# Lending idle streams' PSUM banks in a four-layer graph attention kernel, with a shorter subtraction and transposes tile by tile

## The chip, the cores and the metric

The kernel runs on one core of a Trainium2 chip. The metric is the device time of one execution in microseconds (us), from the start of the program to its end. Times of one kernel are given as the median of several executions.

## The reference

The input is `x`, 32 graphs of 512 nodes with 256 features, and one adjacency matrix of 512 x 512 for all of them. Four layers follow each other; all arithmetic is in 32-bit floats. In every layer the nodes are normalised, clipped at zero, sent through an attention over the graph, and added back:

```python
h = jnp.maximum(_layernorm(x, axis=-1), 0.0)
x = x + _L0_gnn_ref(h, adj, L0_gnn_W, L0_gnn_a)
# layers 1, 2, 3 in the same way

def _layernorm(x, axis=-1, eps=1e-5):
    m = jnp.mean(x, axis=axis, keepdims=True)
    v = jnp.var(x, axis=axis, keepdims=True)
    return (x - m) / jnp.sqrt(v + eps)

def _L0_gnn_ref(h, adj, W, a):          # layers 1 and 2 differ in slope, heads and output function
    Wh = jnp.einsum('bnf,fo->bno', h, W)
    s_i = Wh @ a1
    s_j = Wh @ a2
    e = jax.nn.leaky_relu(s_i[:, :, None] + s_j[:, None, :], negative_slope=LEAKY_ALPHA)
    e = jnp.where(mask[None, :, :], e, -jnp.inf)
    attention = jax.nn.softmax(e, axis=-1)
    h_prime = jnp.einsum('bij,bjo->bio', attention, Wh)
    return jax.nn.elu(h_prime)
```

Layer 2 has four heads of 64 features. Layer 3 is a chain: a dense layer to 512 features, an attention over all nodes without a mask, a dense layer back to 256 features, and an attention with the mask.

## The kernel before

**Tiles and stages.** One graph is a batch `b`. Its nodes lie on the 128 partitions, in four tiles of 128 nodes (`NT = 4`); its 256 features make two blocks of 128 (`KF = 2`). Per layer the stages are:

- `norm` (L255 to L277), for two node tiles at a time: mean and variance on DVE (L262, L263), the inverse deviation `rs` on ACT (L265, L266), and then `xn` on DVE. With `late` set, which is so after layers 0 and 1, `xn` is max(x - mean, 0) in one instruction with two operations (L269), and the factor `rs` is applied later, in `values`. Without it, `xn` is (x - mean) * rs (L273).
- `turn_pair` (L277 to L283): four transposes on TensorE (L70) bring two node tiles of `xn` into one PSUM tile `b`, and one ACT instruction evicts them with relu into `hT` (L283). The two loops run over feature blocks outside and over the two node tiles inside.
- `values` (L301 to L318): per node tile two matmuls (L66) into a PSUM tile, evicted by ACT with the exponential of the scores (L312, L315) and a scaled copy (L313, L318) into `v`.
- `weights`: four transposes spread a column of `v` over the partitions, and DVE makes the four tiles of attention weights `w` (L346).
- `averages` and `aggregate`: matmuls of `w` and `v` into a PSUM tile, which ACT evicts after a reciprocal on DVE (L380): L414, L415 and L433 in layers 0 and 1, L692 and L693 at the end of layer 3.

In layer 3 the attention without a mask is done by sorting (`sort_attend`), with indirect DMAs issued by POOL (L600, L648) and prefix sums on DVE (L618 to L639) and TensorE (`tot`, `before`). Only the last batch does it by plain matmuls (`attend`).

**Streams.** Four streams (`NS = 4`) work on different batches at the same time: stream i takes the batches i, i + 4, i + 8 and so on. A stream is a Python generator that stops at points where its next work would have to wait, and yields an estimated due time. At build time a loop takes the stream with the smallest due time, and so writes down the program order. Stream i begins at `i * LEAD`, with `LEAD = 75`. A fifth generator, `setup`, is woven into the start: it transposes the adjacency mask (`own` to `maskT`) and prepares the weights of the later layers (`finish_w` and `project`: transposes of a weight, a copy `wT` on ACT at L114, two to four matmuls, a copy on DVE at L120). From the program order the language's scheduler makes a fixed order for each engine, in which an instruction can be put ahead of one whose inputs or whose buffer it expects later. [...]

**PSUM.** All PSUM tiles come from one helper. There are eight tiles, and each stream has two of its own, under a tag that only this stream uses:

```python
def bank():
    return psum.tile([P, N], FP, tag=f"b{turn[0]}", name="b", bufs=8 // NS)
```

`turn[0]` is the number of the stream whose code is being written down; while `setup` runs it is 3, and in the loop over `own` it goes 3, 2, 1, 3. A stream that has not begun, or that has ended, leaves its two tiles unused.

Of the kernel before, what the change touches and what calls it, by code (L numbers as in the profile page):

```python
# [19 lines left out]
FP = mybir.dt.float32  # L20
# [4 lines left out]
OP = mybir.AluOpType  # L25
# [3 lines left out]
P = 128  # L29
# [6 lines left out]
def fast(ctx, tc, flag, x, adj, w0, a0, w1, a1, w2, a2, mlp1_w, mlp1_b, mlp2_w, mlp2_b,  # L36
         w_fc, a_fc, w_hand, a_hand, out):
    nc = tc.nc
    B, N, F = x.shape
    NT = N // P  # L40
    KF = F // P
# [4 lines left out]
    NS = 4  # L46
# [6 lines left out]
    psum = ctx.enter_context(tc.tile_pool(name="psum", bufs=1, space=bass.MemoryType.PSUM))  # L53
    dram = ctx.enter_context(tc.tile_pool(name="dram", bufs=1, space=bass.MemoryType.DRAM))

    turn = [0]
# [11 lines left out]
    def transpose(p, x, i, tied=False):  # L68
        spent[0] += 2 * P
        instruction = nc.tensor.transpose(p, x, i)  # L70
        if tied:
            tc.keep_in_program_order(instruction)

    def bank():
        return psum.tile([P, N], FP, tag=f"b{turn[0]}", name="b", bufs=8 // NS)


    nc.scalar.preload_act_table_set("natural_log_exp_and_others")
# [28 lines left out]
    def project(dst, block, k, a_cols):  # L107

        ft, n = a_cols.shape[1], a_cols.shape[2]
        p = bank()  # L110
        for f in range(ft):
            transpose(p[:, f * P:(f + 1) * P], block(k, f), ident)
        wT = work.tile([P, N], FP, tag="y", name="wT", bufs=3)
        nc.scalar.copy(wT[:, :ft * P], p[:, :ft * P])  # L114
        q = bank()
        for f in range(ft):
            matmul(
                q[:, :n], wT[:, f * P:(f + 1) * P], a_cols[:, f, :], start=(f == 0), stop=(f == ft - 1)
            )
        nc.vector.tensor_copy(dst, q[:, :n] if len(dst.shape) == 2 else q[:, :n].rearrange("p (h c) -> p h c", c=3))  # L120
# [79 lines left out]
    def setup():  # L200
# [7 lines left out]
        for j in range(NT):  # L208
            turn[0] = NS - 1 - j % (NS - 1)
            p = bank()  # L210
            for t in range(NT):
                transpose(p[:, t * P:(t + 1) * P], own[:, t, j * P:(j + 1) * P], ident, j + t == 0)
            nc.scalar.copy(maskT[:, j, :], p)
# [36 lines left out]
    def small(shape, name):  # L250
        return work.tile([P] + shape, FP, tag=name, name=name, bufs=2 * NS)
# [4 lines left out]
    def norm(xt, xn, rs, t0, late):  # L256


        st = small([2, 6], "st")
        mv = small([2, 2], "mv")  # L260
        for i in range(2):
            nc.vector.bn_stats(st[:, i, :], xt[:, t0 + i, :])  # L262
            nc.vector.bn_aggr(mv[:, i, :], st[:, i, :])  # L263
        rp = rs[:, t0:t0 + 2]
        nc.scalar.activation(rp, mv[:, :, 1], AF.Ln, bias=eps)  # L265
        nc.scalar.activation(rp, rp, AF.Exp, scale=-0.5)  # L266
        for i in range(2):
            if late:
                nc.vector.tensor_scalar(  # L269
                    xn[:, t0 + i, :], xt[:, t0 + i, :], mv[:, i, 0:1], 0.0, op0=OP.subtract, op1=OP.max  # L270
                )
            else:
                nc.vector.tensor_scalar(  # L273
                    xn[:, t0 + i, :], xt[:, t0 + i, :], mv[:, i, 0:1], rp[:, i:i + 1], op0=OP.subtract, op1=OP.mult
                )

    def turn_pair(xn, hT, t0):  # L277
        p = bank()
        for k in range(KF):
            for i in range(2):  # L280
                c = (k * 2 + i) * P
                transpose(p[:, c:c + P], xn[:, t0 + i, k * P:(k + 1) * P], ident)
        nc.scalar.activation(hT[:, :, t0 * P:(t0 + 2) * P], p.rearrange("p (k n) -> p k n", k=KF), AF.Relu)  # L283

    def turned(xn, when):

        hT = work.tile([P, KF, N], FP, tag="hT", name="hT", bufs=3)
        turn_pair(xn, hT, 0)
        yield when
        turn_pair(xn, hT, 2)  # L290
        yield after_us(0.6)
        return hT
# [114 lines left out]
    def layer0(xt, xn, rs, when):  # L407
        v, wt = yield from plain((yield from turned(xn, when)), W0)
        xn, rs = new_xn(), small([NT], "rs")
        for t0 in range(0, NT, 2):  # L410
            r, q = pair(), pair("q")
            for i in range(2):
                p, rd = averages(v, wt, t0 + i)
                nc.scalar.activation(q[:, i, :], p, AF.Exp, scale=rd)  # L414
                nc.scalar.activation(r[:, i, :], p, AF.Relu, scale=rd)  # L415
                if i == 0:
                    yield after_us(0)
            add_elu(xt[:, t0:t0 + 2, :], r, q)
            norm(xt, xn, rs, t0, True)
            last, when = when, after_us(6)  # L420
            if t0 == 0:
                yield after_us(0)
        yield last
        return xn, rs, when

    def layer1(xt, xn, rs, when):
        v, wt = yield from plain((yield from turned(xn, when)), W1, rs)
        xn, rs = new_xn(), small([NT], "rs")
        for t0 in range(0, NT, 2):
            r = pair()  # L430
            for i in range(2):
                p, rd = averages(v, wt, t0 + i)
                nc.scalar.activation(r[:, i, :], p, AF.Relu, scale=rd)  # L433
                if i == 0:
                    yield after_us(0)
            xr = xt[:, t0:t0 + 2, :]
            nc.vector.tensor_tensor(xr, xr, r, op=OP.add)
            norm(xt, xn, rs, t0, True)
            last, when = when, after_us(5)
            if t0 == 0:  # L440
                yield after_us(0)
        yield last
        return xn, rs, when

    def layer2(xt, xn, rs, when):
# [56 lines left out]
        for t0 in range(0, NT, 2):  # L502
            norm(xt, xn, rs, t0, False)
# [244 lines left out]
    while ready:  # L748
        i = min(ready, key=ready.get)
        if i == NS:  # L750
            turn[0] = NS - 1
            ready[i] += 4.0
            if next(early, early) is early:
                del ready[i]
            continue
        turn[0], spent[0] = i, 0.0
        begun[0] = ready[i]
        wait = next(streams[i], None)
        if wait is None:
            del ready[i]  # L760
        else:
            ready[i] = wait

# [409 lines left out]
@with_exitstack  # L1173
def kernel(ctx: ExitStack, tc: tile.TileContext, *args):
    nc = tc.nc
    keep = ctx.enter_context(tc.tile_pool(name="keep", bufs=1))
    flag = keep.tile([1, 1], I32, name="flag")
    fast(tc, flag, *args)
    bad = nc.values_load(flag[0:1, 0:1], min_val=0, max_val=1)
    with tc.If(bad > 0):  # L1180
        general(tc, *args)
# [27 lines left out]
```

## The time and the profile before

| | |
|---|---|
| median of three executions | 2951.32 us (2948.66 to 2954.25) |
| the profiled execution | 2955.39 us |
| its span, first to last instruction | 2953.7 us |
| TensorE matmuls (PE) busy | 2870.6 us (97%) |
| DVE busy | 2224.6 us (75%) |
| ACT busy | 1538.9 us (52%) |
| POOL busy | 497.2 us (17%) |
| mean granted TensorE clock | 0.994 |

The profile shows one execution, the profiled one, which took 4.07 us more than the median. PE stands for matmuls and transposes on TensorE, PEld for the loading of their stationary operand, DVE for VectorE, ACT for ScalarE, POOL for GpSimd, SP for the engine that issues most DMAs. A line such as L66 is the line of the kernel: L66 is the helper that issues all matmuls, L70 the one that issues all transposes. "Idle before" is the time in which an engine did nothing ahead of an instruction, put down to what released it. PEclk is the clock granted to TensorE, as a share of its full speed.

### The profile page before, as it was taken

What the parts mean: (1) busy time and instruction counts of PE and PEld (TensorE: products, weight loads), DVE (VectorE), ACT (ScalarE), POOL (GpSimd) and SP (SyncE); (2) the same over time, 40 slices, a digit from 0 to 9 for tenths busy, and PEclk for the clock granted to TensorE, in tenths of its full rate; (3) what the DMA queues carried; (4) which work ended last, traced back from release to release, by engine and by line L of the source; (5) the groups of instructions that cost most, each with busy time, mean ns of one, the idle gap of its engine ahead of it and who ended that gap; (6) DMA issues with size and microseconds to landing.
All of it is one profiled execution on the core that took longest, in us unless ns stands there. A gap on an engine that the chain in (4) does not pass through costs nothing.

```text
span 2953.7 us, 43083 instructions
## 1 busy us (share of the span) xinstructions
PE 2870.6 (97%) x15177; PEld 2329.4 (79%) x15177; DVE 2224.6 (75%) x5674; ACT 1538.9 (52%) x3918; POOL 497.2 (17%) x509
## 2 busy tenths in 40 slices
PE   7999999999999999999999999999999999999998
PEld 5778888778887877888778888778878778887765
DVE  4578878778878777878778777787777788777763
ACT  3445555554555555555545555545555555555544
POOL 0011122111122121121111121111121111221120
PEclk9999999999999999999999999999999999999999
DMA  3033233233232332233332232222232322332330
GB/s 93 12 100 95 83 98 115 82 99 98 83 101 96 99 101 91 85 106 94 101 94 87 87 115 92 96 97 91 87 116 90 98 94 86 94 115 76 98 108 16
DMA packets 193150, 270.89 MB, mean 92 GB/s; under 512 B 16992, under 2 KB 156062, under 8 KB 192928
## 3 DMA queue, kind: packets, MB, share of 16 engines
q1 hardware_dynamic: 163168, 169.76, 18.4%
q0 software_dynamic: 29760, 98.30, 10.2%
q8 instruction: 123, 2.02, 0.3%
q14 instruction: 99, 0.81, 0.1%
HBM read 152.62 MB, written 115.39 MB: 91 GB/s over the span
## 4 chain that ended last, share of the span: by engine, by line
PE 80%; DVE 12%; ACT 5%; issue 1%; DMA 1%; POOL 0%; SPq 0%; POOLq 0%; ACTq 0%; DVEq 0%
PE b L66 72%; PE b L70 7%; DVE st L262 3%; DVE xn L273 1%; DVE xn L269 1%; DVE sums L634 1%; ACT v L318 1%; DVE sums L625 1%; DVE x L399 1%; ACT rs L265 1%; DVE y L398 1%; DVE mv L263 1%; DVE y L703 1%; ACT y L498 1%; ACT q L497 0%
## 5 line engine op out<-in xcount | busy, mean ns | idle before, releaser
L66 PE MATMUL b<-v,w 128*128 128x65 f32 (+1 forms) x7232 | 1221.6, 321 | 11.0 <-DVE w L346 8.5
L66 PEld LDWEIGHTS b<-v,w 128*128 128x128 f32 x7232 | 1050.1, 191 | 175.1 <-issue 66.0
L66 PE MATMUL b<-WFC,oT 128*128 128x256 f32 (+1 forms) x2048 | 499.6, 381 | 3.0 <-ACT ends L521 3.0
L66 PEld LDWEIGHTS b<-WFC,oT 128*128 128x128 f32 x2048 | 375.0, 190 | 52.0 <-ACT v L522 3.4
L66 PE MATMUL b<-W,hT 128*128 128x259 f32 (+1 forms) x1536 | 384.6, 389 | 5.0 <-ACT v L318 4.4
L346 DVE SCALAR_TENSOR_TENSOR w<-b,v,maskT 128x512 f32<-128x512 f32 x512 | 370.2, 747 | 4.6 <-PE b L70 3.4
L600 POOL DMA_INDIRECT order<-v,at x248 | 280.3, 1130 | 490.2 <-DVE oT L719 152.4
L66 PEld LDWEIGHTS b<-W,hT 128*128 128x128 f32 x1536 | 284.8, 191 | 55.7 <-ACT v L318 10.7
L346 DVE SCALAR_TENSOR_TENSOR w<-spread,v,maskT 128x512 f32<-128x512 f32 x384 | 270.1, 746 | 0.0
L380 DVE RECIPROCAL rden<-b 128x1 f32<-128x1 f32 (+1 forms) x516 | 79.6, 166 | 252.6 <-PE b L66 250.8
L706 POOL TENSOR_TENSOR x<-x,y 128x512 f32<-128x512 f32 x64 | 81.1, 1268 | 1076.3 <-ACT y L704 962.8
L66 PE MATMUL b<-hT,WM 128*128 128x512 f32 x512 | 249.1, 597 | 0.7 <-ACT hT L283 0.7
L648 POOL DMA_INDIRECT g<-table,at x124 | 121.2, 977 | 732.5 <-ACT y L668 380.9
L66 PE MATMUL b<-oT,WM 128*128 128x512 f32 x512 | 231.4, 595 | 0.0
L522 ACT ACTIVATE v<-b,ends 128x256 f32<-128x256 f32 x256 | 119.0, 468 | 179.0 <-PE b L66 174.5
L262 DVE BATCH_NORM_STATS2 st<-x 128x6 f32<-128x256 f32 x512 | 192.9, 408 | 5.2 <-DMA x<-in_x_dram 2.6
L283 ACT ACTIVATE hT<-b 128x512 f32<-128x512 f32 x256 | 147.2, 592 | 91.3 <-PE b L70 91.2
L332 ACT ACTIVATE oT<-b,bias 128x512 f32<-128x512 f32 x128 | 87.8, 686 | 195.4 <-PE b L66 195.4
L405 DVE TENSOR_TENSOR y<-q,y 128x512 f32<-128x512 f32 x192 | 132.7, 691 | 67.4 <-ACT q L404 66.5
L70 PE MATMUL b<-ident,xn 128*128 128x128 f32 x1024 | 154.9, 279 | 23.9 <-DVE xn L273 18.0
L66 PEld LDWEIGHTS b<-oT,WM 128*128 128x128 f32 x512 | 97.6, 191 | 95.8 <-issue 92.5
L70 PEld LDWEIGHTS b<-ident,xn 128*128 128x128 f32 x1024 | 125.4, 144 | 59.8 <-DVE xn L273 33.5
(142 smaller groups left out, 3749.1 us busy)
## 6 DMA issues: line engine op xcount, KB each, us to landing
table<-sums SPq DMA_DIRECT2D x62, 1032.0 KB
sums<-order SPq DMA_DIRECT2D x62, 516.0 KB
spread<-row SPq DMA_DIRECT2D x96, 256.0 KB
x<-in_x_dram SPq DMA_DIRECT2D x32, 512.0 KB
out_dram<-x SPq DMA_DIRECT2D x64, 256.0 KB
sums<-order SPq DMA_DIRECT2D x62, 129.0 KB
order<-v,at POOLq DMA_INDIRECT x248, 2.9
g<-table,at POOLq DMA_INDIRECT x124, 4.7
```

The source lines that it names most:

```text
L66: nc.tensor.matmul(p, w, x, **flags)
L70: instruction = nc.tensor.transpose(p, x, i)
L262: nc.vector.bn_stats(st[:, i, :], xt[:, t0 + i, :])
L283: nc.scalar.activation(hT[:, :, t0 * P:(t0 + 2) * P], p.rearrange("p (k n) -> p k n", k=KF), AF.Relu)
L332: nc.scalar.activation(o[:, f, :], p, AF.Relu, bias=bias[:, f:f + 1])
L346: w = nc.vector.scalar_tensor_tensor(wt[:, j, :], r, t_col(j), maskT[:, j, :], op0=OP.max, op1=OP.mult)
L380: nc.vector.reciprocal(r, den)
L405: nc.vector.tensor_tensor(r, q, r, op=OP.add)
L522: nc.scalar.activation(halves[c][:, t, :F], ps[:, :F], AF.Copy, scale=ends[:, t, 0:1])
L600: nc.gpsimd.indirect_dma_start(out=orders[c], out_offset=bass.IndirectOffsetOnAxis(ap=at[:, 0, t:t + 1], axis=0), in_=halves[c][:, t, :], ...
L648: nc.gpsimd.indirect_dma_start(out=g, out_offset=None, in_=table, in_offset=bass.IndirectOffsetOnAxis(ap=at[:, 1, t:t + 1], axis=0),)
L706: nc.gpsimd.tensor_tensor(xr, xr, y, op=OP.add)
```

## The change

Four edits, all in `fast`:

1. `bank` hands out PSUM tiles from the stream's own tag and, in turn, from the tags of all streams that are not active. A stream counts as active from the first time that the loop takes it until its generator ends. `setup` is never counted. While all four streams are active, a stream gets its own tag only, as before.
2. With `late` set, `xn` is x - mean alone; the clip at zero that it had is left to the relu in the eviction of `turn_pair`, which was there before.
3. The loops of `turn_pair` are exchanged: both transposes of the first node tile come first, then both of the second.
4. The loop that takes the streams keeps the set `active`.

```diff
+    active = set()
+    banks = [0]
+
     def bank():
-        return psum.tile([P, N], FP, tag=f"b{turn[0]}", name="b", bufs=8 // NS)
+
+        own = [turn[0], *(i for i in range(NS) if i not in active and i != turn[0])]
+        banks[0] += 1
+        return psum.tile([P, N], FP, tag=f"b{own[banks[0] % len(own)]}", name="b", bufs=8 // NS)
...
             if late:
                 nc.vector.tensor_scalar(
-                    xn[:, t0 + i, :], xt[:, t0 + i, :], mv[:, i, 0:1], 0.0, op0=OP.subtract, op1=OP.max
+                    xn[:, t0 + i, :], xt[:, t0 + i, :], mv[:, i, 0:1], None, op0=OP.subtract
                 )
...
     def turn_pair(xn, hT, t0):
         p = bank()
-        for k in range(KF):
-            for i in range(2):
+        for i in range(2):
+            for k in range(KF):
                 c = (k * 2 + i) * P
                 transpose(p[:, c:c + P], xn[:, t0 + i, k * P:(k + 1) * P], ident)
...
         begun[0] = ready[i]
+        active.add(i)
         wait = next(streams[i], None)
         if wait is None:
             del ready[i]
+            active.remove(i)
         else:
             ready[i] = wait
```

## The prediction

> **What bounds the kernel now.** I read the busy shares first, then stretches of the span, then the waits of TensorE in each stretch, then the timeline around the longest ones. The page says that matmuls fill the span:
>
> ```profile
> PE 2870.6 (97%) x15177; PEld 2329.4 (79%) x15177; DVE 2224.6 (75%) x5674; ACT 1538.9 (52%) x3918; POOL 497.2 (17%) x509
> ```
>
> The change adds and removes no matmul, so it can only touch the 83 us in which PE is idle, and the time lost to a lower TensorE clock. Four stretches show where these lie (start : end and length, then busy us of each engine with instruction counts, then PEclk):
>
> ```profile
> 0.00:225.00 225.00, 195.58 (x1030) 160.19 (x1031) 135.65 (x388) 95.05 (x257) 17.51 (x26) 0.95 0.22 69
> 225.00:2800.00 2575.00, 2542.26 (x13539) 2070.95 (x13538) 2006.76 (x5107) 1375.29 (x3513) 457.53 (x463) 1.00 0.30 95
> 2800.00:2944.20 144.20, 132.77 (x611) 98.27 (x610) 80.34 (x178) 67.41 (x149) 20.92 (x19) 0.96 0.20 64
> 2944.20:2953.70 9.50, 0.00 (x0) 0.00 (x0) 1.80 (x4) 1.12 (x2) 1.26 (x1) 0.61 0.14 45
> ```
>
> PE idles 29.4 us while the streams start (0 to 225 us), 32.7 us in the 2575 us when all four run (1.3%), 11.4 us while they end, and 9.5 us behind the last matmul. Only the start and the end have idle streams, and only there is the clock below full. The waits of PE in the first 225 us (us in total, times, longest):
>
> ```profile
> PE b L66 <- DVE w L346: 4.4, 5, 2.6
> PE b L66 <- DVE tot L622: 3.4, 1, 3.4
> PE b L66 <- DVE W0a L104: 2.9, 1, 2.9
> PE b L70 <- ACT rs L265: 2.6, 1, 2.6
> PE b L66 <- ACT wT L114: 2.5, 5, 0.7
> PE b L70 <- DVE xn L269: 2.4, 1, 2.4
> ```
>
> Most are waits for data; `wT` L114 is ACT, through which the preparation of the weights goes, with two banks at a time. [...] Here are the stretch with the wait of 2.6 us at 65 us, and the next one:
>
> ```profile
> 64.00:68.00 4.00, 1.35 (x9) 1.03 (x8) 2.87 (x12) 1.81 (x6) 0.00 (x0) 1.00 0.00 0
> 68.00:72.00 4.00, 3.94 (x14) 2.70 (x13) 2.96 (x12) 1.58 (x7) 0.00 (x0) 0.61 0.00 0
> ```
>
> After it the clock is 0.61 for 4 us: (1 - 0.61) x 3.94 = 1.5 us more. Counted in the same way, the start loses 8.5 us of clock (at 28, 44 to 52, 68 and 176 us) and the end 4.9 us (at 2820, 2844 and 2872 us).
>
> [...]
>
> **The change part by part.**
>
> *x - mean in one operation (256 on DVE).* The price is shown by L623, which is a one-operation tensor_scalar with a column scalar, 258 elements:
>
> ```profile
> L623 DVE TENSOR_SCALAR sums<-sums,T x62: 344/350/356, 185.7 to 2847.5; 128x258 f32<-128x258 f32 x62
> L269 DVE TENSOR_SCALAR xn<-x,mv x256: 318/345/1431, 38.0 to 2791.3; 128x256 f32<-128x256 f32 x128
> ```
>
> 350 against 345 ns: no gain (ends: 0.03 us less or more each). Even 256 x 0.03 = 8 us of DVE would lie beside PE, because L269 makes PE wait only once, at 104 us. The relu costs nothing: L283 does it already. I take 0.
>
> *Transposes by tile.* With all four streams running, PE waits 16.3 us in 28 cases for `xn` L273, one per batch. The four L273 follow each other at 0.38 us; a transpose step on PE is about 0.11 us. Where four transposes stand together in the order, the second waits for the second tile today; later the first two run on tile one, which saves 0.11. The built order has this for two of four batches. In one it changes "transpose, matmul, three transposes" to "four transposes, two matmuls", which loses the filler (about 0.13); in one nothing changes. Sum 2 x 0.11 - 0.13 = 0.1 us per four batches, 0.6 us over seven rounds (-1 to +1.5).
>
> *The banks.* The built orders of the two programs agree from about 200 to 2750 us on every engine but for those transposes; SP's order is the same throughout and POOL's nearly so. What moves is the start and the end. I walk along PE's new order with the durations of the trace.
>
> - To 26 us: the weight transposes of `W0` no longer wait for two banks, so the first `values` could start 1.5 us earlier. But the mask needs `adj` (landed 11.3), L203 (1.23) and POOL (1.92), and L346 still stands behind the 2.27 us reduction L219 on DVE. I take 0.5 us of 4.2.
> - 32 to 56 us: the waits for `wT` and for L415 (0.74 + 0.51 + 0.24 + 0.73 + 0.52 = 2.7) are waits for banks, and the clock loses 3.0 there. Six lent banks remove most of it, but eight more weight transposes (0.157) and four more small matmuls (0.29) now stand ahead of stream 0's last aggregates: 2.4 us later for its chain. From +5.7 to -2.4; I take 3.0.
> - 65 us: two matmul groups of layer 2 (0.87) go into the wait of 2.65, splitting it in two short ones[...]. 0.9 to 2.4; I take 1.4.
> - 102 to 109 us: four groups of stream 1's `values` (4 x 0.43) go ahead of the transposes that wait 2.41 and 1.22. I take 1.7 (0 to 3).
> - 173 us: one `values` group goes ahead of the wait of 3.37 for `tot`, one during it (0.87), and DVE makes `tot` ahead of L399. The next transposes then wait for L269 as before. I take 1.5 (0.5 to 4, with the clock).
>
> Sum of the start 8.1. A stall that is filled can return at the next data wait, so I count 6 (0 to 13). It then carries to the end: in the middle PE is the bound, and its short waits depend on DVE and ACT work just before.
>
> - The end. At 2837 PE waits 0.66 for a bank; the order now has all eight matmuls of that stage in a row (0.4). At 2869.9 it waits 2.97 for a bank behind ACT L521; a fourth group (1.73) fits now, but the gathers (4.7 us to landing) feed the transposes of `y` behind it, so I count 1.0 (0 to 4). At 2938 and 2940.8 the last two groups wait 0.69 and 0.73 for banks, and a transpose group (0.44) stands between; now four groups follow each other. The last one ends some 2.4 us earlier and the eviction chain with it; I take 2.0.
>
> Sum of the end 3.4 (1 to 7).
>
> **Sum:** 6 + 3.4 + 0.6 + 0 = 10 us. Against the profiled execution, 2955.4 - 10 = 2945.4; that one lies 4.07 above the median, so for the median 2951.3 - 10 = **2941.3 us**.
>
> **Rivals.**
> 1. *Idle streams' banks hide little.* The start is bound by stream 0's chain through DVE and ACT: of the six waits shown, five are for DVE or for `rs`. Then only the end counts: 3.4 + 0.6 - 1 = 3 us, 2948 us. For it speaks that work put into a wait for data doesn't end that wait; against it, that the lent banks let another stream's work in, which is then gone later.
> 2. *Slower: lent work blocks PE's queue.* At 32 to 45 us the weight preparation goes ahead of stream 0's aggregates (2.4 us); two matmul groups ahead of layer 2's aggregates at 100 us and again at 173 us add 0.87 each, and a lent bank that is evicted late makes its owner wait. If this chain sets the start, it loses 4.1 us[...]: 7.3 us, with nothing won at the end, 2958 us. It decides once stream 0's delay is larger than the 2.7 us of bank waits removed.
> 3. *Clock kept.* [...]most of the 8.5 us of clock comes back too: 13 + 5 = 18 us, 2933 us.
>
> **How the numbers follow.** A difference of 0.2%, 5.9 us, is about what a measurement of this kernel can tell from no change. Chances: forecast 0.55, clock kept 0.15, little hidden 0.22, slower 0.08. Half-way between forecast and rival 1 is the bound for "faster" (2945.4), so a small part of each falls on the other's side: faster 0.70, same 0.22, slower 0.08. The range from 2932 to 2951 holds the forecast, its unknown ends, rival 1 and most of rival 3.
>
> **What would show it.** In the profile after: the middle stretch idles PE 32 us again; L269 keeps a median near 345 ns; the waits for `wT` L114 nearly vanish; those of 2.65, 2.41 and 3.37 us shrink and the clock at 44 to 52 us is near full; at the end the waits for L693, L703 and L312 are gone, that for L521 is below 1.5 us. I am wrong if the four streams' middle changes length by more than 3 us, if stream 0's second layer starts later than at 57 us, or if waits for lent banks appear.

## The result and the profile after

| | before | after |
|---|---|---|
| median, ten executions each | 2952.47 us | 2942.65 us (2940.53 to 2945.59) |
| ratio after to before | | 0.9966 [0.9959, 0.9974] |
| the profiled execution, and its span | 2955.39, 2953.7 us | 2945.59, 2943.9 us |
| mean granted TensorE clock | 0.994 | 0.995 |

In square brackets stand 95% intervals, in round ones the lowest and the highest execution. The change gains 10 us of 2952. Beside the experiments the changed kernel was run again: 0.9975 [0.9965, 0.9985], 7.4 us. The two together give about 9 us.

Code lines of the changed kernel lie 6 higher than those of before: L346 is L352, L269 is L275, L273 is L279, L312 and L318 are L318 and L324, L405 is L411. The page's line of busy times, and then the stretches of the profiled execution after (start : end, length, busy us of PE, PEld, DVE, ACT, POOL with counts, PEclk):

```profile
PE 2863.2 (97%) x15177; PEld 2326.1 (79%) x15177; DVE 2224.0 (76%) x5674; ACT 1537.4 (52%) x3918; POOL 501.3 (17%) x509
```

```profile
0.00:225.00 225.00, 200.97 (x1088) 165.72 (x1089) 143.51 (x407) 97.50 (x264) 20.28 (x28) 0.98 0.23 71
225.00:2800.00 2575.00, 2540.87 (x13527) 2069.05 (x13526) 2004.73 (x5104) 1378.82 (x3521) 459.30 (x463) 1.00 0.30 96
2800.00:2934.40 134.40, 121.36 (x566) 91.39 (x564) 74.36 (x163) 60.00 (x134) 20.47 (x18) 0.96 0.19 63
```

The same 15177 matmul records are there. In the first 225 us PE now does 1088 of them and not 1030, and idles 24.0 us in place of 29.4. In the middle it idles 34.1 us (32.7 before). The waits of PE in the first 225 us after (us in total, times, longest):

```profile
PE b L66 <- ACT hT L289: 5.3, 9, 0.9
PE b L66 <- DVE w L352: 5.2, 6, 2.7
PE b L70 <- DVE xn L279: 2.9, 4, 1.2
PE b L70 <- DVE xn L275: 2.5, 4, 1.1
PE b L66 <- ACT wT L120: 0.5, 2, 0.3
```

The single long waits for `tot` (3.4) and `rs` (2.6) are gone, and in their place stand many short ones: nine for `hT`, none above 0.9 us. The timeline of PE shows how the old waits of 2.65, 2.41 and 3.37 us look now:

```profile
61.12 1.17 PE L66 MATMUL b<-W,hT 128*128 128x268 f32 x4 [0.82 <-ACT hT L289]
62.86 0.70 PE L70 MATMUL b<-ident,xn 128*128 128x128 f32 x4 [0.57 <-DVE xn L275]
64.25 1.17 PE L66 MATMUL b<-W,hT 128*128 128x268 f32 x4 [0.69 <-ACT hT L289]
...
100.36 0.70 PE L70 MATMUL b<-ident,xn 128*128 128x128 f32 x4 [0.70 <-DVE xn L275]
101.98 2.02 PE L66 MATMUL b<-W,hT 128*128 128x259 f32 x8 [0.92 <-ACT hT L289]
...
170.60 0.44 PE L70 MATMUL b<-ident,xn 128*128 128x128 f32 x2 [1.06 <-DVE xn L275]
```

Each wait is cut into pieces with work between them. The two stretches that answer to those of 64 to 72 us before keep the full clock behind 1.83 us of idle time:

```profile
60.00:64.00 4.00, 2.17 (x11) 1.15 (x9) 3.43 (x14) 2.07 (x6) 0.00 (x0) 1.00 0.02 4
64.00:68.00 4.00, 3.75 (x20) 2.93 (x21) 3.10 (x10) 2.56 (x9) 0.00 (x0) 1.00 0.00 0
```

**One pair of profiles misleads.** Read alone, this pair puts 8.3 us ahead of batch 4 (it begins at 390.80 and not at 399.14 us) and some 2 us at the end; the expectations below, written from this pair, take 8.5 and 2.4. But the profiled execution before had a late transfer at its very beginning (PE waits 2.9 us for `W0a`), and the one after had one at its end, as shown below. The experiments gave twelve more profiles, in which most stages occur both with and without lending. I therefore cut each into four stages that begin at the same instruction in all of them, and leave out what stands ahead of the first: the first transpose of `own`, the 32 aggregates of stream 0's second layer, and SP's transfer of `row` (one for each batch) for batch 4 and for batch 31. The table has the mean, and the lowest and highest of each group in brackets, in us.

| stage | banks not lent in it | banks lent in it | difference | forecast |
|---|---|---|---|---|
| `own` to stream 0's second layer | 41.1 (5 profiles, 40.7 to 41.4) | 40.0 (6, 37.7 to 42.8) | -1.1 | -3.0 |
| second layer to batch 4 | 342.4 (6, 342.0 to 342.8) | 338.2 (8, 336.2 to 340.2) | -4.2 | -4.6 |
| batch 4 to batch 31 | 2404.0 (6, 2403.4 to 2404.4) | 2404.9 (8, 2403.5 to 2405.6) | +0.9 | -0.6 |
| batch 31 to the end | 149.7 (6, 148.5 to 151.5) | 145.1 (8, 142.3 to 148.3) | -4.6 | -3.4 |

For batch 4 to 31 a kernel counts as lent if its streams borrowed at the start. In the first row `no_setup` counts as not lent, since its preparation keeps to two banks, and the three kernels with an early reduction, below, are left out. The sum is -9.0 us, which is the time measured. The split between the first two rows is less firm than their sum: in `after_again` and `end_two` the first stage loses 6.8 us to a lower clock and the second none, in `banks_only` it is 2.6 and 3.4. (The clock's loss is half of PE's busy time while the granted clock is 0.50: in a row of matmuls of 257 columns the next one then follows after 0.428 us in the median of the first profile after, and after 0.217 at 1.00.) The forecast of the first two stages is its parts 3.0, and 1.4 + 1.7 + 1.5.

### The profile page after: what moved, and what is told of

It is laid out like the page before. It is cut to its first block, busy times and chain, and to the rows that moved or that the text cites. A ratio compares the mean times of both kernels' runs of the same rounds, so it can differ in the third digit from the quotient of the medians.

```text
span 2943.9 us, 43065 instructions
## 1 busy us (share of the span) xinstructions
PE 2863.2 (97%) x15177; PEld 2326.1 (79%) x15177; DVE 2224.0 (76%) x5674; ACT 1537.4 (52%) x3918; POOL 501.3 (17%) x509
## 3 DMA queue, kind: packets, MB, share of 16 engines
q0 software_dynamic: 29760, 98.30, 10.1%
## 4 chain that ended last, share of the span: by engine, by line
PE 77%; DVE 13%; ACT 5%; DMA 3%; issue 1%; POOL 0%; SPq 0%; POOLq 0%; ACTq 0%; DVEq 0%
PE b L66 70%; PE b L70 7%; DVE st L268 3%; DVE xn L279 1%; DMA order<-v,at 1%; DVE xn L275 1%; DVE sums L640 1%; DVE w L352 1%; ACT v L324 1%; DMA sums<-order 1%; DVE sums L631 1%; ACT y L504 1%; DVE x L405 1%; ACT q L503 1%; DVE y L404 1%
## 5 line engine op out<-in xcount | busy, mean ns | idle before, releaser
L352 DVE SCALAR_TENSOR_TENSOR w<-b,v,maskT 128x512 f32<-128x512 f32 x512 | 369.0, 743 | 4.9 <-PE b L70 3.6
L352 DVE SCALAR_TENSOR_TENSOR w<-spread,v,maskT 128x512 f32<-128x512 f32 x384 | 269.3, 741 | 0.0
L712 POOL TENSOR_TENSOR x<-x,y 128x512 f32<-128x512 f32 x64 | 81.3, 1270 | 1074.9 <-ACT y L710 963.8
L411 DVE TENSOR_TENSOR y<-q,y 128x512 f32<-128x512 f32 x192 | 132.5, 690 | 67.0 <-ACT q L410 66.5
```

Source lines behind the costliest of these rows:

```text
L352: w = nc.vector.scalar_tensor_tensor(wt[:, j, :], r, t_col(j), maskT[:, j, :], op0=OP.max, op1=OP.mult)
L411: nc.vector.tensor_tensor(r, q, r, op=OP.add)
L712: nc.gpsimd.tensor_tensor(xr, xr, y, op=OP.add)
```

## The experiments

All have the kernel before run beside them on the same chip. Theory 1 at the outset was: the gain is the lent banks', mostly at the start (8.5 us), the transposes give 0.6 us, the subtraction nothing. The rivals stand in the expectations.

**The four edits apart.** `banks_only` is the kernel before with edits 1 and 4; `sub_only` and `trans_only` are the kernel before with this alone:

```diff
# sub_only
-                    xn[:, t0 + i, :], xt[:, t0 + i, :], mv[:, i, 0:1], 0.0, op0=OP.subtract, op1=OP.max
+                    xn[:, t0 + i, :], xt[:, t0 + i, :], mv[:, i, 0:1], None, op0=OP.subtract
# trans_only
-        for k in range(KF):
-            for i in range(2):
+        for i in range(2):
+            for k in range(KF):
```

> The kernel before with edits 1 and 4 alone: idle streams' banks are lent; the subtraction keeps its two operations and the transposes their old order. Theory 1 (the lent banks bring the gain at the start and the end, the transposes about 0.6 us, the subtraction nothing): about 9 us below before, 0.5 us above the changed kernel, so 2943 us. Theory 2 (a good part comes from the shorter subtraction or from the order of the transposes): 4 us or more above the changed kernel, 2946 us or more.

> The kernel before with edit 2 alone: x - mean in one operation. Theory 1: no change, within 1.5 us of before; DVE's median of one subtraction stays at 345 ns. Theory 2: 3 us or more below before.

> The kernel before with edit 3 alone: transposes by node tile. Theory 1: 0.6 us below before (-1 to +1.5 gained), which is hardly more than the scatter; stretch 225 to 2800 us with 0.1 us less for each round of four batches. Theory 2: 3 us or more below before.

Measured: `banks_only` 0.9969 [0.9957, 0.9981], 9.2 us below before; `sub_only` 0.9994 [0.9985, 1.0002]; `trans_only` 0.9998 [0.9990, 1.0007]. The lent banks alone give the whole gain. Neither of the other edits gives a difference that the times resolve; the interval of `sub_only` still reaches to 4.4 us below before, so there the trace decides. For the transposes a stage resolves more than the whole: batch 4 to 31 takes 2403.39 us in `trans_only` against 2404.10 and 2404.07 in before and `sub_only`, 0.7 us less, as forecast. But among the other kernels whose streams don't borrow there, the two with edit 3 take 2403.4 (`setup_only`) and 2404.4 us (`end_only`), and the one without it 2404.4 (`before_early`). So 0.6 us fits, and is not shown. The subtraction's rows, of `sub_only` and then of the changed kernel (minimum, median, maximum in ns):

```profile
L269 DVE TENSOR_SCALAR xn<-x,mv x256: 318/344/1434, 35.6 to 2788.8; 128x256 f32<-128x256 f32 x128
```

```profile
L275 DVE TENSOR_SCALAR xn<-x,mv x256: 317/344/1435, 40.6 to 2783.9; 128x256 f32<-128x256 f32 x128
```

One operation less changes the median from 345 to 344 ns, that is, by nothing.

**Start and end apart.** In `start_only` an ended stream stays active; in `end_only` all streams are active from the beginning:

```diff
# start_only
-            active.remove(i)
# end_only
-    active = set()
+    active = set(range(NS))
```

> The changed kernel, but a stream that has ended stays active, so that banks are lent only before a stream begins. Theory 1: the start keeps its 8.5 us and the end loses its 2.4 us: 2945 us, 2.4 us above the changed kernel, with the waits for ACT at the two last groups of the final stage back (0.7 us each). Theory 3 (the end gains nothing on balance, because the bank wait of 2.17 us ahead of `tot` and the lower clock behind it eat it): within 1 us of the changed kernel.

> The changed kernel with all four streams counted as active from the beginning, so that banks are lent only after a stream has ended. Theory 1 (start and end add up: all of the lending gave 9.2 us, the start's share alone 4.8): 4.4 us below before. Theory 4 (they don't add up: time gained at the start is lost again at the end unless the end lends too): 2 us or less below before. The start shows the waits of before (2.6 us at 65 us, 3.4 us for `tot` at 173 us).

Measured: `start_only` 0.9984 [0.9977, 0.9991], 4.8 us below before (2949.26 against 2954.11 us); `end_only` 0.9982 [0.9975, 0.9989], 5.3 us. The first expectation missed: the end is worth as much as the start, and the split of the first pair of profiles falls. The second holds: 4.8 and 5.3 make 10.1 us, so within their intervals the two add up, and nothing gained at the start is lost again at the end.

The last stage shows best what the end gains. The four groups of eight aggregates on PE, and an instruction of the eviction chain on DVE, in the kernel before and in the changed one:

```profile
2932.57 4.32 PE L66 MATMUL b<-v,w 128*128 128x257 f32 x16 [0.98 <-DVE w L346]
2938.02 2.00 PE L66 MATMUL b<-v,w 128*128 128x257 f32 x8 [0.69 <-ACT y L693]
2940.76 2.00 PE L66 MATMUL b<-v,w 128*128 128x257 f32 x8 [0.73 <-DVE y L703]
2943.51 0.43 DVE L403 TENSOR_SCALAR q<-q 128x512 f32<-128x512 f32 x1 [0.54 <-ACT q L692]
```

```profile
2924.66 7.21 PE L66 MATMUL b<-v,w 128*128 128x257 f32 x32 [0.45 <-DVE w L352]
...
2932.58 1.26 POOL L712 TENSOR_TENSOR x<-x,y 128x512 f32<-128x512 f32 x1 [11.57 <-ACT y L710]
2932.89 1.23 DVE L409 TENSOR_SCALAR q<-q 128x512 f32<-128x512 f32 x1 [0.17 <-ACT q L698]
```

With other banks free the 32 matmuls run in one row. From the first of them to the end of the last the kernel before takes 2942.76 - 2932.57 = 10.2 us, the changed one 7.2: 3.0 us less. To the end of the span it is only 21.1 against 19.2, 1.9 us less. The evictions now come closer together, and DVE's L409 (L403 before) runs into POOL's L712: 1.23 us and not 0.43. It is 1.23 in the second profile of the changed kernel and in `banks_only` too, with L712 beginning 0.31 to 0.32 us ahead of it in all three, and 0.43 in `start_only`, whose L712 begins 2.01 us ahead and is done. This takes 0.8 of the 1.1 us that are lost again behind PE.

The other part of the end's gain lies in the 46 us ahead of this stage. From the first of the last 32 matmuls `b<-oT,WM` (2886.38 us before, 2881.13 after) to the 32 aggregates it takes 46.19 us in all six profiles without lending at the end and 43.53 to 43.55 in all eight with it: 2.65 us less for 182 matmuls in each, at full clock. Waits of PE there add up to 1.9 us before and to 0.5 after. Two of those before, which are gone:

```profile
2915.53 2.00 PE L66 MATMUL b<-v,w 128*128 128x257 f32 x8 [0.26 <-ACT y L693]
2927.51 3.50 PE L66 MATMUL b<-WHA,rT 128*128 128x259 f32 x14 [0.49 <-ACT rT L332]
```

From batch 31 to that point the two groups take 82.4 and 82.3 us on average, the second with four transposes (0.44 us) more: hardly a gain.

**A second profile of the changed kernel.**

> The changed kernel once more, for a second profile and on the chip of the next three. 9 to 10 us below before. Theory A (the bank wait of 2.17 us ahead of `tot` at 2831 us, with the lower clock behind it, comes with the built order): the wait is there again, over 1.5 us. Theory B (it comes from a gather that landed late in that one run): the wait is under 0.5 us, and batch 31 to the end takes 144 us and not 148.

Measured: 0.9975 [0.9965, 0.9985], 7.4 us; from batch 31 to the end 143.9 us, where the first profile took 148.3. The bank wait of 2.17 us ahead of `tot` is gone. Lines of PE, DVE and ACT of the first profile, in which `tot` (PE) waits for an eviction on ACT that stands behind L503, which waits for `y` of L496 on DVE, which stands behind L626, which waits for a gather:

```profile
2827.72 0.43 DVE L626 TENSOR_TENSOR sums<-sums 128x258 f32<-128x258 f32 x1 [2.34 <-DMA sums<-order]
2829.19 0.63 ACT L503 ACTIVATE q<-y 128x512 f32<-128x512 f32 x1 [6.82 <-DVE y L496]
2830.90 0.92 PE L66 MATMUL b<-tot,before 128*128 128x258 f32 x2 [2.17 <-ACT v L318]
```

And of the second, where the gather came 1.0 us earlier, although PE was 1.1 us later at the matmuls ahead of `tot`:

```profile
2826.76 0.43 DVE L626 TENSOR_TENSOR sums<-sums 128x258 f32<-128x258 f32 x1 [0.95 <-DMA sums<-order]
2828.23 0.63 ACT L503 ACTIVATE q<-y 128x512 f32<-128x512 f32 x1 [4.77 <-DVE y L496]
2829.94 0.70 PE L66 MATMUL b<-tot,before 128*128 128x258 f32 x2
```

Both signs of Theory B came true: it was one late gather. From its issue to L626 it took 5.1 us in the first profile, 3.7 in the second and 3.3 to 4.7 in the six others that lend at the end. The bank that `tot` was waiting for had been handed out, and the queues of DVE, ACT and PE carried the delay on: these instructions stand in the same order in both profiles, and L626, L503 and `tot` are each 0.96 us later in the first.

**Who borrows at the start.** In `no_setup` the preparation of mask and weights keeps to its own tag, and in `setup_only` it alone borrows:

```diff
# no_setup: preparing[0] is True only while setup is written down
+        own = own[:1] if preparing[0] else own
# setup_only
+        own = own if preparing[0] else own[:1]
```

> The changed kernel, but the preparation of mask and weights keeps to its own two banks; the streams still borrow. Theory 1 (the part of 32 to 56 us in the sum, the waits for `wT` and the clock there, is half of the start's gain): 3 us above the changed kernel, waits for `wT` of 0.5 to 0.7 us back (2.5 us in all). Theory 5 (the preparation was only ahead or behind in the same queue; the start is bound by stream 0's chain, and what helps is the streams' own borrowing at 65, 102 and 173 us): within 1 us of the changed kernel.

> The changed kernel, but only the preparation of mask and weights borrows; the streams keep to their own two banks throughout, at the end too. Theory 1 (waits for `wT` and the clock at 32 to 56 us are half of the start's gain): 3 us below before and 0.6 more from the transposes, 3.6 us. Theory 5 (only the streams' own borrowing helps at the start): 0.6 us below before, with the waits of 2.65 us for rs, 2.41 us for xn and about 3 us for tot as before.

Measured: `no_setup` 0.9969 [0.9957, 0.9981], 9.2 us below before and so equal to the changed kernel within some 4 us, which alone doesn't exclude the 3 us of Theory 1; `setup_only` 0.9998 [0.9990, 1.0006], 0.6 us below before. The forecast of 3.6 us for `setup_only` lies outside its interval (3.0 below to 1.8 above), and Theory 5 fits both kernels. Waits of PE in the first 225 us of `setup_only`:

```profile
PE b L66 <- DVE tot L630: 2.9, 1, 2.9
PE b L70 <- ACT rs L273: 2.6, 1, 2.6
PE b L70 <- DVE xn L277: 2.4, 1, 2.4
PE b L66 <- ACT wT L122: 2.3, 5, 0.5
```

The waits at 65, 102 and 173 us are all there. So are five waits for `wT`, 2.3 us in all against 2.5 before, though the preparation has six more banks; only the wait of 0.74 us for L415 is gone. Lent to the streams alone, in `no_setup`, the waits for `wT` grow to 4.9 us. Only where both borrow do they nearly go (0.5), because other work then stands between a copy and the matmul that needs it. But even that gains little: in the changed kernel waits for `hT`, `v`, `maskT` and `xn`, some 2 us in all from `own` to the second layer, stand in their place. And `no_setup`, in which PE idles 8.1 us there, more than in any other profile, loses only 1.4 us of clock, less than any other; so its waits cost no time that the runs resolve.

The second layer to batch 4 tells the same: 342.3 us in `setup_only`, 338.4 in `no_setup`. The idle time of PE in that stage is 15.0 to 15.8 us in the six profiles whose streams don't borrow, and 12.2 to 12.7 in the eight others; the clock's loss is 4.2 to 4.8 us against 0 to 3.4. The stage begins with the 32 aggregates of stream 0's second layer, which show that part of what two banks cost isn't seen as idle time. In `end_only`, whose streams keep two banks here, and in the changed kernel:

```profile
53.55 7.79 PE L66 MATMUL b<-v,w 128*128 128x257 f32 x32 [0.94 <-DVE w L352]
```

```profile
52.66 7.21 PE L66 MATMUL b<-v,w 128*128 128x257 f32 x32 [0.85 <-DVE w L352]
```

The row takes 7.79 us in `setup_only` too and 7.21 in `no_setup`, so it is the stream's own borrowing that shortens it, by 0.6 us. The trace shows where: DVE finishes the four tiles of `w` 0.66 us apart. With two banks PE does two matmuls with each tile and then waits for the next one: in the kernel before, whose row begins at 56.77 us and takes 7.79 us as well, tiles are ready at 57.29, 57.95 and 58.60 us, and every second matmul starts right behind, at 57.34, 58.00 and 58.66. With more banks it does four matmuls with each tile, which take 0.87 us, and DVE keeps ahead. The page counts these short waits as busy.

**Lending at the end only later.** In `end_two` nothing is lent while just one stream has ended:

```diff
+        own = own[:1] if len(ended) == 1 else own
```

> The changed kernel, but at the end banks are lent only once two streams have ended. Theory A: `tot` stands ahead of part of the eight matmuls of layer 3 again and waits 0.7 us or less, 1.5 to 3 us below the changed kernel. Theory B: nothing gained there, and the wait of 2.9 us for L527 is back: 1 to 2 us above the changed kernel.

Measured: 0.9971 [0.9958, 0.9983], 8.6 us below before, which is the changed kernel's own gain. From batch 31 to the end it takes 142.3 us, the lowest of the eight with lending, but `both_early`, which has the same rule, takes 146.6. Since the wait that it was to remove was one late gather's, this tells nothing more; the wait for L527 did not come back either.

**The stall that is left at the start.** Stream 0's first aggregates wait 2.73 us at 26 us, because the attention weights L352 stand on DVE behind a reduction of the whole adjacency matrix (L225, 2.28 us), which nothing needs so early. `reduce_early` moves it behind the load of the matrix:

```diff
+        tc.keep_in_program_order(nc.vector.tensor_reduce(differ[:, 0:1], adj_sb, AX.XY, OP.min))
         for j in range(NT):
             turn[0] = NS - 1 - j % (NS - 1)
...
-        tc.keep_in_program_order(nc.vector.tensor_reduce(differ[:, 0:1], adj_sb, AX.XY, OP.min))
```

`both_early` is this and `end_two` together; `before_early` is this move in the kernel before.

> The changed kernel with the reduction of the adjacency matrix on DVE (2.27 us, L225) put right behind its load, and so ahead of stream 0's first attention weights by more than the wait. If the stall of 2.73 us at 26 us and the clock of 0.69 and 0.50 behind it (2.6 us) are due to it: 2 to 5 us below the changed kernel, and the wait for w at the first aggregates below 1 us. If DVE is then late with the first normalisation instead, which stands behind the reduction: within 1 us of the changed kernel, with a wait for `xn` of about 2 us ahead of it.

> The changed kernel with both: the reduction of the adjacency matrix right behind its load, and lending at the end only once two streams have ended. If the two add up (6 us at the start, 1 to 2 us at the end): 15 to 16 us below before, 7 us below the changed kernel. If time saved at the end is only moved into the next wait for the gathers: as the kernel with the early reduction, 14 us below before. Profile: first wait for w 0.8 us, waits for `y` L411 at the end two and not four.

> The kernel before with the early reduction alone, nothing lent. Theory 1 (without lent banks PE has nothing to put into the waits at 65, 102 and 173 us, but the first stall is the same DVE reduction in both kernels): 4 to 6 us below before, so that the two changes add up. Theory 6 (what is gained ahead of 30 us is taken back by the bank waits of the preparation at 32 to 56 us): 2 us or less below before.

Measured: `reduce_early` 0.9952 [0.9938, 0.9966], 14.2 us below before; `both_early` 0.9954 [0.9941, 0.9967]; `before_early` 0.9993 [0.9985, 1.0001], 2.1 us. The lines of DVE and PE, of the changed kernel and of `reduce_early`:

```profile
23.47 2.28 DVE L225 TENSOR_REDUCE differ<-adj 128x1 f32<-128x2048 int32 x1
25.66 2.72 DVE L352 SCALAR_TENSOR_TENSOR w<-b,v,maskT 128x512 f32<-128x512 f32 x4
26.46 2.94 PE L66 MATMUL b<-v,w 128*128 128x257 f32 x6 [2.73 <-DVE w L352]
```

```profile
10.10 2.28 DVE L214 TENSOR_REDUCE differ<-adj 128x1 f32<-128x2048 int32 x1
22.05 2.73 DVE L352 SCALAR_TENSOR_TENSOR w<-b,v,maskT 128x512 f32<-128x512 f32 x4 [0.21 <-PE b L70]
22.85 2.87 PE L66 MATMUL b<-v,w 128*128 128x257 f32 x12 [0.84 <-DVE w L352]
```

The wait falls from 2.73 to 0.84, and this kernel is 5.8 us faster than the changed one run beside it (2938.42 against 2944.18 us; five and nine executions, so the size is rough). From `own` to the second layer PE idles 3.7 us, where the kernels with lending idle 5.1 to 6.3. So about 2 us of the gain are seen; the rest may be the clock or lie within the two intervals. `both_early`, 13.6 us below before, is no faster than `reduce_early`, and four waits for `y` stand at the end, not two: the later lending adds nothing. In the kernel before, Theory 6 gave the right size, but its mechanism is not seen. 1.85 us of the first wait go; from 32 to 56 us the waits for `wT` stay at 2.0 us and the one for `y` grows from 0.7 to 1.0. The one profile even keeps 3 us up to batch 4; it is of one of the fastest of 14 executions, so the interval, which reaches to 4.4 us, leaves open how much is kept.

## Why the prediction was right, and where not

The time came out as forecast (10 us; 10.0 and 7.4 measured), by the mechanism that it names: work of other streams goes into the waits of the start and the end. That the sum fits so well is partly luck, because terms that were too large and gains that it did not have make up for each other. By its steps:

- **The subtraction at nothing: right.** A row of another line with one operation was enough to price it.
- **The transposes at 0.6 us: not contradicted**, 0.7 us in `trans_only`, but the kernels that share the stage scatter by 1 us.
- **To 26 us, 0.5: not seen.** The first aggregates begin at 23.6 to 24.4 us in `sub_only`, `trans_only` and `end_only`, and at 23.6 to 26.5 in the five profiles in which streams and preparation borrow and the reduction is late; before and `sub_only`, which do not differ there, lie 2.5 us apart.
- **The preparation at 32 to 56 us, 3.0: wrong**, 1.1 us. That the waits for `wT` and L415 would go came true; that the time would go with them did not. The banks were only part of the reason for `wT`, other waits took their place, and idle time from `own` to the second layer is 6.3 to 6.4 us in before, `sub_only`, `trans_only` and `end_only`, and 5.1 to 6.3 with lending. The clock's loss, 4.5 to 4.9 us in those four, scatters from 2.6 to 8.2 with lending: it did not hang on these waits (see the last section).
- **65, 102 and 173 us, 1.4 + 1.7 + 1.5 = 4.6: right as a sum**, 4.2 us measured for the stage, 3 of them idle time. Its parts are not: cut at the transfers of `row` for batches 1 and 2, the first two waits gave 1.7 us (3.1 forecast) and the third 2.8 (1.5). Behind the wait for `tot` the clock lost 2.5 to 3.1 us in all six profiles without the streams' borrowing, and nothing in seven of the eight with it.
- **The discount from 8.1 to 6: right in kind**, for 5.3 us measured in the two stages. Filled waits did return, but in the preparation, and not at 65 to 173 us.
- **The middle: wrong sign.** Kernels whose streams borrowed at the start take 0.9 us more from batch 4 to 31. Five of the eight have a wait of 0.8 to 1.8 us for L318 or its neighbours at 963 to 971 us, and take 2404.8 to 2405.6; the three without it (`banks_only`, `no_setup`, `both_early`) take 2403.5 to 2404.7, about as the kernels without lending do. What makes the wait was not tried.
- **The end at 3.4: too small**, 4.6 us, and half of it elsewhere. The last stage gave 1.9 (2.0 forecast). The 1.4 for the waits at 2837 and 2870 us came to at most 0.5; the other 2.65 come from the 46 us ahead of the last stage, to which the sum gave nothing. That a filled wait comes back at the gathers was right. Three of four waits for `y` in the changed kernel:

```profile
2866.27 0.63 PE L70 MATMUL b<-ident,y 128*128 128x128 f32 x4 [1.65 <-DVE y L411]
2869.82 0.66 PE L70 MATMUL b<-ident,y 128*128 128x128 f32 x4 [1.20 <-DVE y L411]
2875.26 0.63 PE L70 MATMUL b<-ident,y 128*128 128x128 f32 x4 [1.76 <-DVE y L411]
```

The four, 5.1 us in all and 3.6 in the second profile, take the place of the one wait of 2.97 us for L521, which is gone. Of the signs named, the waits for `wT` nearly vanish and those for L693 and L703 are gone as said, stream 0's second layer starts at 52.7 us, before 57, and a new wait for a bank did appear, ahead of `tot`, in one of the two profiles.

- **The sign "clock near full at 44 to 52 us": not reliable.** The same instructions in the same order, in the first and in the second profile of the changed kernel:

```profile
44.00:48.00 4.00, 3.28 (x18) 2.56 (x19) 2.32 (x9) 1.91 (x8) 0.00 (x0) 1.00 0.00 0
48.00:52.00 4.00, 3.39 (x17) 2.28 (x15) 0.77 (x6) 2.43 (x7) 0.00 (x0) 1.00 0.01 2
```

```profile
44.00:48.00 4.00, 3.95 (x13) 2.67 (x14) 1.66 (x8) 1.40 (x5) 0.00 (x0) 0.50 0.00 0
48.00:52.00 4.00, 4.00 (x12) 2.98 (x12) 0.23 (x2) 1.45 (x4) 0.00 (x0) 0.50 0.00 0
```

The profile before already spoke against a clock that falls only behind long waits. It fell to half for 6.8 us at 45 us, where the longest wait of the 14 us ahead is 0.74 us.

Rival 3 (clock kept) came true in part: in the first 225 us the clock is at half for 20.5 us in before, `sub_only`, `trans_only` and `end_only`, and for 10.2 to 13.7 us in the changed kernel's two profiles, `banks_only` and `end_two`; `no_setup` has 6.8 and `setup_only` 17.1. In `start_only` it is 23.9, and its 17 executions reach from 2943.7 to 2954.4 us, at clocks of 0.996 to 0.992. That the clock hangs on the longest wait is not shown: this rival's 18 us, the 1.5 us of clock weighed at 65 us in the forecast, and 3.2 us in Rival 2's 7.3 were my estimates from the falls of the one profile before.

Rival 1 had its premise right for the preparation, where lending gave about 1 us and the early reduction on DVE gave more. It fell on the later waits. Rival 2 did not come about: stream 0's second layer was not delayed.

## What to carry to other kernels

A wait that looks like a wait for a buffer may be one for data, and a wait that goes may make room for another one: lend the buffer to the part that waits alone, and look at the stage's time and not at the wait. Before a gain is split by stages from two profiles, cut several profiles of kernels that share a stage at the same instruction; the scatter of one execution (a late transfer, a fall of the clock) was here as large as each part. And look on the waiting engine's queue for work that nobody needs yet: one reduction moved gave some 6 us on top of the lending, and 2 in the kernel before.

## What the runs showed of the hardware

- The granted clock of TensorE is 1.00 or 0.50 in the traces of before and after, and nothing between; a 0.61 over 4 us is a mean. No stretch that was summed in the other twelve profiles has a mean below 0.50. Except for the last fall of a run (9.39 and 8.85 us), each fall of before and after lasts 3.41, 6.83 or 10.24 us. In each of the two all falls begin on one grid of 3.41 us, at 27.92 us plus whole steps in before and at 25.49 us plus whole steps in after.
- Long waits are not what the falls have in common. In `after_again` the clock fell at 43.8 us for 10.2 us, when in the 14 us ahead PE had two waits only, of 0.29 and 0.47 us. What goes with the falls is how much the matmuls stream within one step of the grid. In a row, a matmul of 257 columns follows the last one after 0.216 us. Counted at that rate for each column, the step ahead of this fall (40.4 to 43.8 us) is filled to 0.33, because 14 of its 22 matmuls have three columns only; they count as busy on the page (2.00 of the 2.00 us from 40 to 42 us). In the first profile the grid cuts the same instructions elsewhere, the steps are filled to 0.52 and 0.51, and the clock stays. Of the 1700 steps at full clock between 13 us and the end in the traces of before and after, the 12 ahead of a fall are filled to 0.00 to 0.37, and the 1688 that the clock survives to 0.38 or more. Over all fourteen traces the two groups overlap: 8 of the 76 steps ahead of a fall are filled to 0.366 to 0.42, and the least filled step that the clock survives to 0.366. This is read from the traces; no run varied it.
- A tensor_scalar on DVE of 128x512 took 1.23 us beside a GpSimd tensor_tensor (L409 at 2932.89 us, L712 at 2932.58, in after), and 0.43 alone (L409 at 2929.14 us). In the traces of before and after 21 of the 256 subtractions `xn<-x,mv` (L269, L275) took more than 0.6 us (345 and 344 ns are the medians), all of them beside a GpSimd tensor_tensor (L706, L712). 7 and 8 others that run beside one for 0.29 to 0.30 us took 0.32 to 0.45.
- In a row of matmuls of 257 columns the next one follows after 0.215 to 0.220 us; behind one that had to wait for `w` it follows after 0.29 to 0.32 (before from 56.77 us, the changed kernel from 52.66 us).
- PE's order was the same in both profiles of the changed kernel, whatever each waited for: the 384 matmuls and transposes of the second from 5 to 90 us stand in the same order in the first.
